# Paged attention with a conditioned residual: scores with the keys on the partitions, sums from a ones column, no maximum, remade tables

## The chip, the cores and the metric

One core of one Trainium2 chip runs the whole program in one launch. The metric is device time in microseconds (us) of one execution; less is better. All tensors are float32.

## The reference, cut to what matters

There are 64 batches of 32 new tokens, width 512. Two residual parts are added to x one after the other: a 32 x 32 mixing of a batch's tokens, chosen by a condition, and grouped-query attention over a paged cache (32 query heads, 8 key/value heads, head width 128, 16 pages of 32 keys for each batch).

```python
x = x + einsum('bct,bcd->bdt', x, L0_weights[condition])
q, k, v = x Wq^T, x Wk^T, x Wv^T            # by heads of 128
q, k = rope(rmsnorm(q) * wq), rope(rmsnorm(k) * wk)   # positions: cached length + 0..31
k_all = concat([k_cache[block_table], k])   # 512 cached keys, 32 new ones
v_all = concat([v_cache[block_table], v])
valid = concat([arange(512) < cached length, ones(32)])
scores = where(valid, q k_all^T / sqrt(128), -1e30)
x = x + (softmax(scores) v_all) Wo^T
```

The conditions, block table and cached lengths (207 to 1644) are inputs; the norm weights lie between 0 and 1; the cached keys and values are normal random numbers.

## The kernel before, in words

The tokens are worked on in 16 tiles of 128 (four batches), and the heads in two halves (four key/value heads, sixteen query heads), so that a half's weights stay on chip: 32 steps, `st.hh` the half and `st.t` the tile. A pair is one batch and one key/value head: 4 query heads x 32 tokens = 128 queries. A step has four batches (`bt`) of four pairs (`g`), 16 slots.

For a pair, `scores` (L407) multiplies the queries (stationary) with 512 cached keys (L414) and 32 new ones (L415) into one PSUM tile, queries on the partitions. One VectorE instruction adds the mask, scales and takes the minimum of the negated scores (L421); ScalarE takes the exponential and the sum (L425); VectorE takes the reciprocal (L427) and multiplies (L428). A slot later `transpose_p` (L431) turns the probabilities over on TensorE, four blocks of 128 keys (L434) and one of 32 (L437), and ScalarE copies them out (L439, L440). Another slot later `values` (L442) multiplies the value tiles (stationary) with them, four times 128 keys (L448) and the 32 new ones (L451), and VectorE copies the output into `ot` (L452).

Beside a step's attention, `pieces` (L469) does the next step's projections, one piece a slot: the mixing (`x1_a`, L251, L271), its transposes (`x1_b`, L274), keys (`k_a`, `k_b`), values (`v_a`) and four groups of queries (`q_a`, `q_b`). Each projection is four matmuls of 512 columns (L303); `norm_rope` (L308) norms and rotates on VectorE with squares on ScalarE (L313) and a power on POOL (L320); `transposed` (L344) turns heads over (L347). `out_proj` (L383, L387) of the step before stands in slot 2.

`load_kv` (L153) fetches a batch's keys by 16 DMAs of one page each on SP's queue (L167; the pages of the input are already stored transposed, 128 x (heads, 32 keys)) and its values by four indirect gathers on POOL's queue (L174). Both tiles have two buffers. Weights come through POOL's queue (L143). The angles' sines and cosines of all tiles are made at the start (L211 to L229). Each engine works in its own order; the order of instructions on it is the framework's, which follows the program with small shifts.

Of the kernel before, what the change touches and what calls it, by code (L numbers as in the profile page):

```python
# [19 lines left out]
P = 128  # L20
B, S, HID = 64, 32, 512  # batches, new tokens of each, width
D, HQ, HK = 128, 32, 8  # head width, query heads, key/value heads
REP = HQ // HK  # query heads to one key/value head
PAGES, PSIZE, NPP = 64, 32, 16
L = NPP * PSIZE  # cached keys that a batch looks at
LK = L + S  # all its keys
NCOND = 16
BT = P // S  # batches in a tile of 128 tokens
NT = B // BT  # tiles of tokens
NHH = 2  # the heads are worked on in two halves, so that a half's weights stay on chip  # L30
GH = HK // NHH  # key/value heads in a half
QH = GH * REP  # query heads in a half
KC = HID // P  # chunks of the width
VC = L // P  # chunks of the cached keys
# [4 lines left out]
PSLOT = P // PSIZE  # pages in a chunk of 128 keys  # L39

TWO_PI = 2.0 * math.pi
C1 = 6.28125  # 2 pi in three parts, the first two short enough for exact products
C2 = float((np.float32(TWO_PI - C1).view(np.uint32) & np.uint32(0xFFFFF000)).view(np.float32))
C3 = TWO_PI - C1 - C2
ROUND = 12582912.0  # 1.5 * 2**23: adding it rounds to an integer
PI_IN = 3.1415925  # the largest float32 below pi
# [3 lines left out]
def cond_resid_paged_attention_kernel(  # L50
    ctx: ExitStack,
    tc: tile.TileContext,
    x: bass.AP,  # [B*S, HID]
    cond: bass.AP,  # [P, NT]: condition of a token's batch
    lens: bass.AP,  # [P, NT]: cached length of a token's batch
    lens_row: bass.AP,  # [1, B]
    pages: bass.AP,  # [B, NPP]: block table
    pages_v: bass.AP,  # [P, B*VC]: page of each cached key, by chunks of 128 keys
    w_cond: bass.AP,  # [NCOND*S, S]
    wq: bass.AP,  # [HID, HQ*D]  # L60
    wk: bass.AP,  # [HID, HK*D]
    wv: bass.AP,  # [HID, HK*D]
    wo: bass.AP,  # [HQ*D, HID]
    qn_w: bass.AP,  # [1, D]
    kn_w: bass.AP,  # [1, D]
    kt: bass.AP,  # [NHH, PAGES, D, GH*PSIZE]: cached keys, transposed page by page
    vc: bass.AP,  # [PAGES*PSIZE*NHH, GH*D]: cached values
    inv_freq: bass.AP,  # [1, D/2]
    out: bass.AP,  # [B*S, HID]
):  # L70
    nc = tc.nc
    HD = D // 2

    def pool(name, bufs, **kw):
        return ctx.enter_context(tc.tile_pool(name=name, bufs=bufs, **kw))

    const = pool("const", 1)
    wpool = pool("weights", 1)
    kv = pool("kv", 2)
    act = pool("act", 2)  # L80
    work = pool("work", 2)
    small = pool("small", 4)
    ps_s = pool("ps_s", 1, space=PSUM)
    ps_t = pool("ps_t", 2, space=PSUM)
    ps_o = pool("ps_o", 2, space=PSUM)
    ps_p = pool("ps_p", 2, space=PSUM)
    dram = pool("dram", 1, space=DRAM)

# [1 line left out]
    cond_sb = const.tile([P, NT], I32, tag="cond", name="cond_sb")  # L90
    nc.sync.dma_start(cond_sb, cond)
    lens_sb = const.tile([P, NT], I32, tag="lens", name="lens_sb")
    nc.sync.dma_start(lens_sb, lens)
# [3 lines left out]
    nc.sync.dma_start(pages_v_sb, pages_v)  # L97
    lens_all_i = const.tile([P, B], I32, tag="lens_all_i", name="lens_all_i")
    nc.sync.dma_start(lens_all_i, lens_row.partition_broadcast(P))

    row_i = const.tile([P, 1], I32, tag="row_i", name="row_i")
    nc.gpsimd.iota(row_i, pattern=[[0, 1]], base=0, channel_multiplier=1)
    nc.vector.tensor_scalar(row_i, row_i, S - 1, None, ALU.bitwise_and)
    row = const.tile([P, 1], F32, tag="row", name="row")  # partition mod 32
    nc.vector.tensor_copy(row, row_i)

    cond_idx = const.tile([P, NT], I32, tag="cond_idx", name="cond_idx")
    nc.vector.tensor_scalar(cond_idx, cond_sb, float(S), row, ALU.mult, ALU.add)
    v_idx = []
    for hh in range(NHH):  # L110
        base = const.tile([P, 1], F32, tag=f"v_base{hh}", name=f"v_base{hh}")
        nc.vector.tensor_scalar(base, row, float(NHH), float(hh), ALU.mult, ALU.add)
        idx = const.tile([P, B * VC], I32, tag=f"v_idx{hh}", name=f"v_idx{hh}")
        nc.vector.tensor_scalar(
            idx, pages_v_sb, float(PSIZE * NHH), base, ALU.mult, ALU.add
        )
        v_idx.append(idx)
# [15 lines left out]
    wt = {}  # L133

    def load_w(kind, hh, g=0):
        if kind == "q":
            src = wq[:, (hh * QH + g * REP) * D : (hh * QH + (g + 1) * REP) * D]
        elif kind == "o":
            src = wo[(hh * QH + g * REP) * D : (hh * QH + (g + 1) * REP) * D, :]
        else:  # L140
            src = (wk if kind == "k" else wv)[:, hh * GH * D : (hh + 1) * GH * D]
        t = wpool.tile([P, 4, 512], F32, tag=f"w{kind}{g}", name=f"w{kind}{g}_{hh}")
        nc.gpsimd.dma_start(t, src.rearrange("(c p) e -> p c e", p=P))  # L143
        wt[kind, g] = t

    def load_x(t):
        xt = work.tile([P, HID], F32, tag="xt", name=f"xt_{t}")
        nc.sync.dma_start(xt, x[t * P : (t + 1) * P, :])
        return xt

    last_k = []

    def load_kv(hh, b):  # L153
        k_t = kv.tile([P, NPP, GH, PSIZE], F32, tag="k_t", name=f"k_t_{hh}_{b}")
        # Behind the last batch's loads: registers hold one batch's page numbers.
        with ExitStack() as order:
            if last_k:
                order.enter_context(tc.issue_after(last_k[0]))
            _, page = nc.values_load_multi_w_load_instructions(
                pages_sb[b : b + 1, :],  # L160
                engines=[mybir.EngineType.SP],
                min_val=0,
                max_val=PAGES - 1,
                skip_runtime_bounds_check_because="a block table names pages of the cache",
            )
        for j in range(NPP):
            ins = nc.sync.dma_start(  # L167
                k_t[:, j, :, :].rearrange("p g r -> p (g r)"),
                kt[hh, bass.ds(page[j], 1)].rearrange("o d e -> (o d) e"),
            )  # L170
        last_k[:] = [ins.ins]
        v_t = kv.tile([P, VC, GH * D], F32, tag="v_t", name=f"v_t_{hh}_{b}")
        for c in range(VC):
            nc.gpsimd.indirect_dma_start(  # L174
                out=v_t[:, c, :],
                out_offset=None,
                in_=vc,
                in_offset=bass.IndirectOffsetOnAxis(
                    ap=v_idx[hh][:, b * VC + c : b * VC + c + 1], axis=0
                ),  # L180
            )
        return k_t, v_t

    load_cond_weights(0)
    x_next = load_x(0)
    load_w("k", 0)
    load_w("v", 0)
    for g in range(GH):
        load_w("q", 0, g)

# [1 line left out]
    norm_w = {}  # L192
    for name, src in (("q", qn_w), ("k", kn_w)):
        w = const.tile([P, D], F32, tag=f"norm_{name}", name=f"norm_{name}")
        nc.sync.dma_start(w, src.partition_broadcast(P))
        norm_w[name] = w
    freq = const.tile([P, HD], F32, tag="freq", name="freq")
    nc.sync.dma_start(freq, inv_freq.partition_broadcast(P))

    pos = const.tile([P, NT], F32, tag="pos", name="pos")  # L200
    nc.vector.tensor_copy(pos, lens_sb)
    nc.vector.tensor_scalar(pos, pos, row, None, ALU.add)
    lens_all = const.tile([P, B], F32, tag="lens_all", name="lens_all")
    nc.vector.tensor_copy(lens_all, lens_all_i)

# [3 lines left out]
    nc.vector.memset(half_pi, math.pi / 2)  # L209

    tmp0 = kv.tile([P, 2, NT * HD], F32, tag="k_t", name="trig_tmp0")  # L211
    tmp1 = kv.tile([P, 2, NT * HD], F32, tag="v_t", name="trig_tmp1")
    ang, turns, red = tmp0[:, 0, :], tmp0[:, 1, :], tmp1[:, 0, :]
    for t in range(NT):
        nc.vector.tensor_scalar(
            ang[:, t * HD : (t + 1) * HD], freq, pos[:, t : t + 1], None, ALU.mult
        )
    nc.vector.tensor_scalar(turns, ang, 1.0 / TWO_PI, ROUND, ALU.mult, ALU.add)
    nc.vector.tensor_scalar(turns, turns, ROUND, None, ALU.subtract)
    nc.vector.scalar_tensor_tensor(red, turns, -C1, ang, ALU.mult, ALU.add)  # L220
    nc.vector.scalar_tensor_tensor(red, turns, -C2, red, ALU.mult, ALU.add)
    nc.vector.scalar_tensor_tensor(red, turns, -C3, red, ALU.mult, ALU.add)
    nc.vector.tensor_scalar(red, red, PI_IN, -PI_IN, ALU.min, ALU.max)
    nc.scalar.activation(sin.rearrange("p t f -> p (t f)"), red, AF.Sin)
    mag = tmp1[:, 1, :]
    nc.scalar.activation(mag, red, AF.Abs)
    nc.scalar.activation(
        cos.rearrange("p t f -> p (t f)"), mag, AF.Sin, bias=half_pi, scale=-1.0
    )  # L229

# [333 lines left out]
```

## Time and profile before

| | |
|---|---|
| median of 3 runs | 2848.94 us (2848.51 to 2850.21) |
| profiled execution, span from first to last instruction | 2849.0 us |
| granted TensorE clock, mean | 0.995 |
| from L387 of one step to L387 of the next, first half / second half | 87.54 / 86.29 us |
| busy of L448 / L414 / L434 / L451 (TensorE) | 594.0 / 560.1 / 314.6 / 247.4 us |
| mean of L425 (ScalarE), L421, L428 (VectorE) | 748, 722, 518 ns |
| first matmul | 22.17 us |
| DMA moved | 326.46 MB, mean 115 GB/s |

The profile is one execution. Engines are PE (TensorE matmul), PEld (TensorE weight load), DVE (VectorE), ACT (ScalarE), POOL (GpSimd) and SP (the queue that issues most DMAs). Part 2 of the page cuts the span into 40 slices, a digit being the busy share in tenths. The chain that ended last goes back from the last instruction, at each step to what released it, and gives shares of the span by engine and by line. The timeline lists instructions with their start, duration and count; matmuls are pipelined, so their durations overlap, and the distance between starts is the pace. The view of waits says who waited for whom: total us, times, longest.

### The profile page before, as it was taken

To read this page: it belongs to the slowest core of one execution; us is meant where nothing else is said; L and a number is where in the kernel's file an instruction comes from. 1 tells how busy PE (TensorE), PEld (TensorE's weight loads), DVE (VectorE), ACT (ScalarE), POOL (GpSimd) and SP (SyncE) were. 2 spreads that over 40 slices of the span, in tenths; PEclk is the share of its full clock that TensorE was granted. 3 is DMA by queue.
4 is the path that set the end of the run, shared out by engine and by line. 5 is a ranking of instruction groups with operands and counts; after the bars stand their busy time and mean duration, and the time that the engine had idled before them with its cause. 6 is when DMAs were issued, how large, how long until landed. Compare 5 with 4: busy or idle time off the path is not lost.

```text
span 2849.0 us, 42362 instructions
## 1 busy us (share of the span) xinstructions
PE 2793.8 (98%) x13024; PEld 1769.4 (62%) x13024; DVE 1445.3 (51%) x4020; ACT 992.9 (35%) x2421; POOL 849.5 (30%) x1052
## 2 busy tenths in 40 slices
PE   3999999999999999999999999999999999999999
PEld 1566666666666666666666666666666666666666
DVE  3545554545554555544555544455544555444553
ACT  1333343333433333333334333334333333333332
POOL 6222322332322223223333222232232232222231
PEclk8999999999999999999999999999999999999999
DMA  6233433334433334335554333334333343333342
GB/s 232 74 110 106 115 110 103 103 111 116 120 90 114 107 114 115 102 101 156 149 165 131 99 111 111 111 111 118 103 106 113 111 118 110 101 109 111 111 115 69
DMA packets 361058, 326.46 MB, mean 115 GB/s; under 512 B 45824, under 2 KB 308608, under 8 KB 360832
## 3 DMA queue, kind: packets, MB, share of 16 engines
q1 hardware_dynamic: 309824, 159.87, 19.6%
q0 software_dynamic: 51008, 163.88, 19.3%
q8 instruction: 104, 1.70, 0.3%
q14 instruction: 122, 1.00, 0.1%
HBM read 302.60 MB, written 12.58 MB: 111 GB/s over the span
## 4 chain that ended last, share of the span: by engine, by line
PE 97%; POOL 1%; DVE 1%; issue 1%; DMA 0%; ACT 0%; SPq 0%; ACTq 0%; DVEq 0%; POOLq 0%
PE ps L414 18%; PE po L448 17%; PE pp_q L303 16%; PE pout L387 16%; PE ppt L434 8%; PE po L451 7%; PE pp_k L303 4%; PE pp_v L303 4%; PE ps L415 3%; PE pt_q L347 2%; PE po L437 2%; PE pmix L271 1%; PE pt_k L347 1%; POOL w_sel L126 0%; POOL v_t L174 0%
## 5 line engine op out<-in xcount | busy, mean ns | idle before, releaser
L174 POOL DMA_INDIRECT v_t<-in_vc_dram,v_idx x512 | 519.3, 1014 | 684.2 <-PE po L448 542.1
L448 PE MATMUL po<-pts,v_t 128*128 128x128 f32 x4096 | 594.0, 279 | 1.4 <-ACT pts L440 1.4
L439 ACT COPY pts<-ppt 128x512 f32<-128x512 f32 x512 | 298.5, 583 | 760.0 <-PE ppt L434 743.6
L414 PE MATMUL ps<-k_t,qt 128*128 128x512 f32 x1024 | 560.1, 629 | 0.0
L448 PEld LDWEIGHTS po<-pts,v_t 128*128 128x128 f32 x4096 | 519.2, 191 | 37.6 <-issue 15.1
L425 ACT ACTIVATE sm<-sm,nm 128x544 f32<-128x544 f32 x512 | 383.1, 748 | 350.4 <-DVE nm L421 343.1
L421 DVE CUSTOM_DVE_ANT_0 sm<-ps,mask 128x544 f32<-128x544 f32 x512 | 369.9, 722 | 253.4 <-PE ps L415 250.5
L303 PE MATMUL pp_q<-wq,x1t 128*128 128x512 f32 x1024 | 474.7, 607 | 0.0
L387 PE MATMUL pout<-wo,ot 128*128 128x512 f32 x1024 | 451.8, 596 | 0.0
L387 PEld LDWEIGHTS pout<-wo,ot 128*128 128x128 f32 x1024 | 190.7, 190 | 221.2 <-issue 221.0
L434 PEld LDWEIGHTS ppt<-ident,sm 128*128 128x128 f32 x2048 | 250.7, 147 | 118.0 <-issue 106.7
L434 PE MATMUL ppt<-ident,sm 128*128 128x128 f32 x2048 | 314.6, 276 | 0.0
L303 PEld LDWEIGHTS pp_q<-wq,x1t 128*128 128x128 f32 x1024 | 186.6, 192 | 186.1 <-issue 186.1
L415 PEld LDWEIGHTS ps<-kn,qt 128*128 128x128 f32 x1024 | 184.8, 190 | 185.1 <-issue 185.1
L428 DVE TENSOR_SCALAR sm<-sm,rden 128x544 f32<-128x544 f32 x512 | 265.2, 518 | 16.4
L452 DVE COPY ot<-po 128x128 f32<-128x128 f32 x512 | 146.2, 285 | 224.4 <-PE po L451 218.4
L320 POOL TENSOR_TENSOR rs_q<-ms_q,minus_half 128x4 f32<-128x4 f32 x128 | 130.7, 1021 | 425.9 <-DVE ms_q L318 425.7
L451 PE MATMUL po<-pts,vn_b 32*128 32x128 f32 x1024 | 247.4, 321 | 0.0
L317 DVE TENSOR_REDUCE ms_q<-sq_q 128x4 f32<-128x512 f32 x128 | 87.8, 686 | 242.1 <-ACT sq_q L313 204.1
L394 DVE TENSOR_TENSOR acc<-pout,acc 128x512 f32<-128x512 f32 x32 | 22.1, 692 | 353.2 <-PE pout L387 353.2
L451 PEld LDWEIGHTS po<-pts,vn_b 32*128 32x128 f32 x1024 | 149.7, 182 | 67.3 <-issue 13.1
L427 DVE RECIPROCAL rden<-den 128x1 f32<-128x1 f32 x512 | 82.4, 161 | 207.8 <-ACT sm L425 207.3
(87 smaller groups left out, 2357.3 us busy)
## 6 DMA issues: line engine op xcount, KB each, us to landing
k_t<-in_kt_dram SPq DMA_DIRECT2D x2048, 64.0 KB
wq<-in_wq_dram POOLq DMA_DIRECT2D x8, 1024.0 KB
wo<-in_wo_dram POOLq DMA_DIRECT2D x8, 1024.0 KB
v_t<-in_vc_dram,v_idx POOLq DMA_INDIRECT x512
vn_b<-vn POOLq DMA_DIRECT2D x128, 64.0 KB
xt<-in_x_dram SPq DMA_DIRECT2D x16, 256.0 KB
x1t_d<-x1t SPq DMA_DIRECT2D x16, 256.0 KB
acc_d<-acc SPq DMA_DIRECT2D x16, 256.0 KB
```

What stands on the lines that cost most here:

```text
L174: nc.gpsimd.indirect_dma_start(out=v_t[:, c, :], out_offset=None, in_=vc, in_offset=bass.IndirectOffsetOnAxis(ap=v_idx[hh][:, b * VC + c : ...
L303: nc.tensor.matmul(pp, st.x1t[:, c, :], w[:, c, :], start=(c == 0), stop=(c == KC - 1))
L387: nc.tensor.matmul(po, st.ot[:, h, :], wt["o", h // REP][:, h % REP, :], start=(h == 0), stop=(h == QH - 1),)
L414: nc.tensor.matmul(ps[:, 0:L], q, k_t[:, :, g, :], start=True, stop=True)
L415: nc.tensor.matmul(ps[:, L:LK], q, st.kn[:, g, bt * S : (bt + 1) * S], start=True, stop=True)
L421: nc.vector.tensor_tensor_reduce(pr.p, ps, mask, -SCALE, 3.0e38, ALU.add, ALU.min, nm)
L425: nc.scalar.activation(pr.p, pr.p, AF.Exp, bias=nm, scale=-1.0, accum_out=den)
L428: nc.vector.tensor_scalar(pr.p, pr.p, rden, None, ALU.mult)
L434: nc.tensor.transpose(pt[:, c, :], pr.p[:, c * P : (c + 1) * P], ident)
L439: nc.scalar.copy(pr.pt[:, 0:VC, :], pt)
L448: nc.tensor.matmul(o, pr.v_t[:, c, d], pr.pt[:, c, :], start=(c == 0), stop=False)
L451: nc.tensor.matmul(o, pr.vn_b[:, d], pr.pt[0:S, VC, :], start=False, stop=True)
```

## The change

The whole kernel is written anew around other layouts; projections, norms, rotation and output projection are the same instructions.

- **Scores transposed.** `scores` takes 128 cached keys at a time as the stationary operand and the pair's 128 queries as the moving one, four times, so the keys lie on the partitions. ScalarE takes the exponential straight from PSUM, without maximum and without mask. `new_scores`, once a batch, multiplies all 128 new keys of the tile with the queries of the four heads; a bias of -1e30 takes out the other batches' keys.
- **Ones column.** The value rows have a 129th column of ones for each head, so that `values` (probabilities stationary, values moving, 129 columns) gives output and denominator. Cached keys past the length are gathered from a row of zeros (`ZROW`). VectorE divides two heads at once, `turn` turns a batch's four outputs over on TensorE and copies them into `ot`.
- **Tables.** `table_piece` reads the cache of a half in 16 pieces, puts a page's keys in the order (key, head), adds the ones column to the values, and writes both to DRAM (`k_tab`, `v_tab`). The first half's pieces stand before step 0, the second half's in steps 4 to 11, two each. The first four batches are read from the inputs and permuted on chip (`direct`).
- **Checked fallback.** At the end all reciprocals of denominators are held against 1e-15 and 1e15; if one is outside, `run(True)` does the work again, in the manner of the kernel before.
- **Queues and order.** The first half's weights come through ScalarE's queue instead of POOL's, the next half's through POOL's in the last step of the first (`next_half`). Angles are made for tile 0 first. `out_proj` stands in slot 3, and `q_b` of a group three slots behind its `q_a`. The scores' PSUM has two buffers, the projections' three.

```diff
+            k_t = kv.tile([P, L, GH], F32, tag="k_t", name=f"k_t_{hh}_{b}_{uid}")
+            if direct:
+                k_raw = wpool.tile([P, NPP, GH, PSIZE], F32, tag="wo2", name=f"k_raw_{b}")
+                k_to, k_from = k_raw.rearrange("p j g r -> p j (g r)"), kt[hh]
+            else:
+                k_to, k_from = k_t.rearrange("p (j r) g -> p j (r g)", j=NPP), k_tab[hh]
...
+            if direct:
+                permuted(k_t.rearrange("p (j r) g -> p j r g", j=NPP), k_raw)
+            else:
+                for c in range(VC):
+                    nc.gpsimd.indirect_dma_start(
+                        out=v_t[:, c, :, :].rearrange("p g d -> p (g d)"),
...
+        def permuted(to, by_head):
+            nc.vector.tensor_copy(to, by_head.rearrange("p j g r -> p j r g"))
+
+        def table_piece(hh, i):
+            n = PAGES // PIECES
+            raw = work.tile([P, n, GH, PSIZE], F32, tag="stage", name=f"traw{hh}_{i}")
+            nc.sync.dma_start(
+                raw.rearrange("p j g r -> p j (g r)"),
+                kt[hh, i * n : (i + 1) * n].rearrange("j d e -> d j e"),
+            )
+            per = work.tile([P, n, PSIZE, GH], F32, tag="stage", name=f"tper{hh}_{i}")
+            permuted(per, raw)
+            nc.sync.dma_start(
+                k_tab[hh][i * n : (i + 1) * n].rearrange("j d e -> d j e"),
+                per.rearrange("p j r g -> p j (r g)"),
+            )
+            st = work.tile([P, GH, D + 1], F32, tag="stage", name=f"tab{hh}_{i}")
+            nc.gpsimd.memset(st[:, :, D : D + 1], 1.0)
+            nc.sync.dma_start(
+                st[:, :, 0:D],
+                vc.rearrange("(p k h) (g d) -> h k p g d", p=P, h=NHH, g=GH)[hh, i],
+            )
+            nc.sync.dma_start(
+                v_tab[hh][0:ZROW, :].rearrange("(p k) e -> k p e", p=P)[i],
+                st.rearrange("p g d -> p (g d)"),
+            )
...
-        nc.tensor.matmul(ps[:, 0:L], q, k_t[:, :, g, :], start=True, stop=True)
-        nc.tensor.matmul(
-            ps[:, L:LK], q, st.kn[:, g, bt * S : (bt + 1) * S], start=True, stop=True
-        )
...
-        nc.vector.tensor_tensor_reduce(
-            pr.p, ps, mask, -SCALE, 3.0e38, ALU.add, ALU.min, nm
-        )
...
-        nc.scalar.activation(pr.p, pr.p, AF.Exp, bias=nm, scale=-1.0, accum_out=den)
...
-        nc.vector.tensor_scalar(pr.p, pr.p, rden, None, ALU.mult)
...
+        def scores(ba, g):
+            ps = ps_s.tile([P, VC, P], F32, tag="ps", name=f"ps_{ba.name}_{g}")
+            for c in range(VC):
+                nc.tensor.matmul(
+                    ps[:, c, :],
+                    ba.k_t[:, c * P : (c + 1) * P, g],
+                    queries(ba, g),
+                    start=True,
+                    stop=True,
+                )
+            pr = work.tile([P, VC, P], F32, tag="pr", name=f"pr_{ba.name}_{g}", bufs=3)
+            nc.scalar.activation(pr, ps, AF.Exp, scale=SCALE)
+            ba.pr[g] = pr
+
+        def new_scores(ba):
+            ps = ps_n.tile([P, GH, P], F32, tag="psn", name=f"psn_{ba.name}")
+            for g in range(GH):
+                nc.tensor.matmul(
+                    ps[:, g, :], ba.st.kn[:, g, :], queries(ba, g), start=True, stop=True
+                )
+            ba.pn = work.tile([P, GH, P], F32, tag="pn", name=f"pn_{ba.name}")
+            nc.scalar.activation(
+                ba.pn, ps, AF.Exp, bias=new_bias[:, ba.bt : ba.bt + 1], scale=SCALE
+            )
...
-            nc.tensor.transpose(pt[:, c, :], pr.p[:, c * P : (c + 1) * P], ident)
...
-        nc.scalar.copy(pr.pt[:, 0:VC, :], pt)
...
-                o, pr.v_t[:, c, d], pr.pt[:, c, :], start=(c == 0), stop=False
...
-        nc.tensor.matmul(o, pr.vn_b[:, d], pr.pt[0:S, VC, :], start=False, stop=True)
...
+            for c in range(VC):
+                nc.tensor.matmul(
+                    o, ba.pr[g][:, c, :], ba.v_t[:, c, g, :], start=(c == 0), stop=False
+                )
+            nc.tensor.matmul(
+                o, ba.pn[:, g, :], ba.st.vn[:, g, :], start=False, stop=True
+            )
...
+            if g % 2:
+                rd = rden[:, ba.n, g - 1 : g + 1]
+                nc.vector.reciprocal(rd, ba.po[:, :, D])
+                nc.vector.tensor_tensor(
+                    ba.o[:, g - 1 : g + 1, :],
...
+        def turn(ba):
+            pt = ps_p.tile([P, GH, P], F32, tag="pp", name=f"pot_{ba.name}")
+            for g in range(GH):
+                nc.tensor.transpose(pt[:, g, :], ba.o[:, g, :], ident)
+            nc.vector.tensor_copy(
+                ba.st.ot[:, :, ba.bt * S : (ba.bt + 1) * S],
+                pt.rearrange("p g (h s) -> p (g h) s", h=REP),
+            )
...
+        load_w("k", 0, eng=nc.scalar)
+        load_w("v", 0, eng=nc.scalar)
...
+        for i in range(PIECES):
+            table_piece(0, i)
...
+            if st.n in range(4, 12):
+                table_piece(1, 2 * (st.n - 4))
+                table_piece(1, 2 * (st.n - 4) + 1)
...
+    redo = const.tile([1, 1], I32, tag="redo", name="redo")
+    run(False)
+    again = nc.values_load(redo[0:1, 0:1])
+    with tc.If(again > 0):
+        run(True)
```

## The prediction

> **What bounds the kernel now.** I read the page from the top: busy shares, the 40 slices, then the chain of work that ended last.
>
> ```profile
> PE 2793.8 (98%) x13024; PEld 1769.4 (62%) x13024; DVE 1445.3 (51%) x4020; ACT 992.9 (35%) x2421; POOL 849.5 (30%) x1052
> ...
> PE   3999999999999999999999999999999999999999
> ...
> DMA  6233433334433334335554333334333343333342
> ...
> PE 97%; POOL 1%; DVE 1%; issue 1%; DMA 0%; ACT 0%; SPq 0%; ACTq 0%; DVEq 0%; POOLq 0%
> PE ps L414 18%; PE po L448 17%; PE pp_q L303 16%; PE pout L387 16%; PE ppt L434 8%; PE po L451 7%; PE pp_k L303 4%; PE pp_v L303 4%; PE ps L415 3%; PE pt_q L347 2%; PE po L437 2%; PE pmix L271 1%; PE pt_k L347 1%; POOL w_sel L126 0%; POOL v_t L174 0%
> ```
>
> The reader is to see that TensorE is never idle after the first slice, and that the chain is TensorE alone. Only 55 us (2849.0 - 2793.8) have no matmul. So a VectorE or ScalarE instruction that goes is worth nothing by itself, and the change is to be priced in TensorE instructions. The timeline of TensorE in mid-run (start, duration; durations overlap, so I take the distance from one start to the next) gives the price of each:
>
> ```profile
> 1505.46 1.13 PE L414 MATMUL ps<-k_t,qt 128*128 128x512 f32 x2
> 1506.42 0.30 PE L415 MATMUL ps<-kn,qt 128*128 128x32 f32 x2
> 1506.56 0.63 PE L347 MATMUL pt_k<-ident,rope_k 128*128 128x128 f32 x4
> 1507.03 0.60 PE L434 MATMUL ppt<-ident,sm 128*128 128x128 f32 x4
> 1507.47 0.27 PE L437 MATMUL po<-ident,sm 128*32 128x128 f32 x1
> 1507.58 1.06 PE L448 MATMUL po<-pts,v_t 128*128 128x128 f32 x8
> 1508.57 0.48 PE L451 MATMUL po<-pts,vn_b 32*128 32x128 f32 x2
> 1508.98 1.12 PE L414 MATMUL ps<-k_t,qt 128*128 128x512 f32 x2
> ...
> 1524.45 0.83 PE L448 MATMUL po<-pts,v_t 128*128 128x128 f32 x6
> 1525.22 0.48 PE L451 MATMUL po<-pts,vn_b 32*128 32x128 f32 x2
> ```
>
> Every float32 matmul is two instructions, a transpose is one. One pair (four query heads of one batch against one key/value head) costs 0.96 (L414) + 0.14 (L415) + 0.44 (L434) + 0.11 (L437) + 0.99 (L448) + 0.41 (L451) = **3.05 us**. Eight L448 take 0.99, six take 0.77: 0.110 us for each, and 0.11 that goes with the change to the 32-row matmul of L451, whose two take 0.205 each. Sixteen pairs are 48.8 us of a step; the step is 87.54 us in the first half of the heads (distance of two runs of L387 in the chain by time, 341.25 to 428.79), so projections, output and their transposes take the other 38.7, and the change leaves these as they are.
>
> **The change on TensorE, for each pair.** Scores: four matmuls of 128 moving columns in place of one of 512, eight instructions. I take 0.110 each, L448 being the row with the same shape and a new stationary tile each time: 0.88. New keys: one matmul against all 128 tokens of the tile, two instructions: 0.22. Values: five matmuls of 129 columns, all 128 rows deep, ten instructions at 0.110 x 129/128: 1.11; the 32-row matmul and its change-over go. The five transposes of the probabilities go; one transpose of the output comes: 0.11. Sum **2.32 us**, 0.73 less, times 512 pairs = **374 us off**. By the quickest row (transposes, 0.44/4 = 0.1075, for all 21) it would be 2.26, 31 us better; by L448's mean in the chain (17.0% of 2849.0 over 4096 = 0.118) 2.47, 77 us worse.
>
> One operand has no row in this trace: the stationary keys of the scores are now read with a step of four floats (16 bytes), since the table holds the four heads side by side. All stationary tiles of before lie densely (qt, v_t, sm, x1t, ot). Bounds: nothing (a spread-out read has no reason to be quicker than a dense one), or the pace of L451, the nearest row at which a matmul of 128 columns does not get its weights in time: 0.205, so 0.095 x 4096 = 389 us more. I take nothing: L434's stationary tile is fetched in 147 ns (mean) and L448's in 191 ns, both at a pace of 0.11, so a load may last longer than the pace and still be covered by earlier ones. [...]
>
> **Beside TensorE.** VectorE loses L421, L427, L428, L452 and the masks (722 + 161 + 518 + 285 ns a pair, 500 a batch), and gains per two pairs a reciprocal and a 256-element product, per batch one 512-element copy; ScalarE loses L439 and L440 and gains one more exponential a batch. Both were under 52% busy; worth nothing. The exponential (748 ns for 544 elements) of a pair has the values of the last pair and the scores of the next before it is wanted, 1.11 + 0.88 = 1.99 us. The pieces of the next step move to other slots, a head's norm and its transposes three slots apart instead of one; the idle time they could save is the 25 us before L347, most of it in the start. The key loads wait, in SP's view, for buffers rather than the other way round:
>
> ```profile
> SPq L167 <- PE ps L415: 945.9, 123, 14.0
> ```
>
> That is 946 us in which SP stood waiting for TensorE to free a key tile, so a step shorter by 12 us (0.73 x 16) is still fed; DMA goes from 38% to some 45% of its engines.
>
> **The tables.** 32 pieces: load 256 KB, permute on VectorE (0.68, as L337's 512 elements), write, and the same for values without the permute. With two stage buffers the next load waits for the last write. The final output DMA takes about 2.6 us (issued 2846.04, span ends 2849.0), the first DMA in the chain 4.9 (lens_all_i): a piece lasts 2.6 + 0.7 + 2.6 = 6 to 4.9 + 0.7 + 4.9 = 10.5 us. The first four batches do without tables, at the price of VectorE's permute of 2048 elements (some 2.7 us) and four multiplies (0.5 each) a batch. The first half's 16 pieces take 95 to 170 us from about 30 us on, and the fifth batch reads them. Before then TensorE has 16 pairs (37), the next step's projections (some 24) and what the built order puts ahead of the fifth batch's scores: an output projection (13.8), two projections (7), new-key scores; the first scores come at 53 us today, so it arrives at about 145 us. Queued behind these waits: on SP the keys of batches 2 to 4, interleaved with pieces; on VectorE the norms and output copies of steps 0 and 1, which TensorE wants. I take **15 us** of stall, bounds 0 and 70. The second half's pieces, two a step in steps 4 to 11, stand in SP's slack (946 us): 0, if that cover fails up to 10 a step (one piece's duration), 80 in all.
>
> **Start.** The weights move from POOL's queue to ScalarE's, and ScalarE's copy of x1t stands behind the issue of the last query weight, its first square behind that of wo; each waits for a lane that an earlier weight holds. The trace moved 284 GB/s in its first 22 us, so 6 to 8 MB land at 21 to 28 us; the copy ended at 26.8 before. Against that only one tile's sine table is made first, not sixteen (12 us of VectorE ahead of the first projection), and 55 us are idle in the start to be had. I take 0, bounds -30 and +20.
>
> **End.** Two comparisons and a sum over 512 counters (0.5 to 0.7 each), a matmul, a flag read by every engine and a branch: **5 us**, bounds 3 and 10. All engines wait for it, nothing is queued behind it, and the last output DMA runs beside it.
>
> **Sum.** 2849.0 - 374 + 15 + 0 + 5 = **2495 us**; the span stands 0.06 us from the median of the runs, 2848.94, so no correction.
>
> **The forecast and its rivals.**
> (A) The forecast, with the bounds of pace, stall and start: 2440 to 2560. For it: same shapes at a known pace, on the engine that is the chain. 62%.
> (B) The strided keys cost in part, half of the upper bound: 2495 + 195 = 2690. 13%.
> (C) The strided keys cost all of it: 2495 + 389 = 2884, **slower** by 1.2%. It decides from a pace of the score instructions of 0.110 + (2849 - 2495)/4096 = 0.196 us. For it: a load of 191 ns that could no longer overlap; against it: nothing in the trace is strided so, either way. 12%.
> (D) The tables are the bound of the first steps and disturb SP in steps 4 to 11: 70 - 15 + 80 more, about 2630. For it: SP and VectorE take their work in order; against it: the 946 us. 8%.
> (E) The change does not do what it says: a denominator leaves 1e-15 to 1e15 and the exact path runs too: some 2495 + 2900 or more, about 5400. Against it: queries are normalised, with weights between 0 and 1, so a score of 128 products over the root of 128 is of the order of one, and 500 such exponentials sum to hundreds. 3%.
> The rest, 2%, is no change.
>
> About 0.2% is what a measurement of this kernel can tell from no change. Faster by more: A, B and D, 0.83; within: 0.02; slower: C and E, 0.15. The range takes A and D and, with B, must hold 8 in 10: 2440 to 2700.
>
> **What would show it.** Right: the new score line at 0.110 from start to start with PE still over 95%, a step of about 75.8 us (87.54 - 11.7), 128x128 transposes of probabilities gone, idle TensorE only before the fifth batch, a few us of branch at the end. Wrong: a weight load of the scores well above 191 ns with a pace near 0.2 (B, C); gaps of TensorE put down to the table's DMAs or to VectorE's permute (D); lines of the exact path in the trace (E). A step of 75.8 with a longer whole would put the miss in start and tables alone.

## The result and the profile after

The change makes the kernel slower. Median of four runs 2968.96 us (2967.63 to 2969.91) against 2849.57 us (2848.51 to 2850.43) for before on the same chip: ratio **1.0416**, interval 1.0401 to 1.0431. The forecast was 2495. The profiled execution of after took 2968.81 us, its span 2967.0, against 2849.0 before: 118.0 us more.

The page of after, in the parts that answer to those shown of before (busy shares, TensorE's and DMA's slices, the chain by engine and by line):

```profile
PE 2897.4 (98%) x14050; PEld 2269.6 (76%) x14050; DVE 846.9 (29%) x2073; ACT 599.8 (20%) x1020; POOL 814.6 (27%) x949
...
PE   4989999999999999999999999999999999999998
...
DMA  8654555543333334335454333333333333333331
...
PE 95%; DMA 2%; POOL 1%; issue 1%; DVE 1%; SPq 0%; ACT 0%; DVEq 0%; ACTq 0%; POOLq 0%
PE ps_x L573 32%; PE po_x L602 15%; PE pout_x L527 14%; PE pp_q_x L446 14%; PE po_x L605 4%; PE psn_x L588 4%; PE pp_k_x L446 3%; PE pp_v_x L446 3%; PE pt_q_x L490 2%; PE pot_x L624 2%; DMA tab<-in_vc_dram 1%; DMA v_tab<-tab 1%; POOL w_sel L116 1%; PE pt_k_x L490 0%; PE pmix_x L410 0%
```

VectorE and ScalarE lost the instructions that the forecast said they would lose (busy 1445 to 847 us, 993 to 600), and it was worth nothing: TensorE is still the chain. The new score line, L573, holds 32% of it, where L414, the scores of before, held 18%. The other number to stop at is PEld, the weight load: 62% before, 76% now. The groups show where it comes from (busy us, mean ns of one; then idle time before, with its releaser):

```profile
L573 PE MATMUL ps_x<-qt_x,k_t_x 128*128 128x128 f32 x4096 | 1049.0, 397 | 12.0 <-DMA k_t_x<-k_tab 10.0
L573 PEld LDWEIGHTS ps_x<-qt_x,k_t_x 128*128 128x128 f32 x4096 | 1000.7, 327 | 15.1 <-issue 13.4
...
L602 PEld LDWEIGHTS po_x<-v_x,pr_x 128*128 128x128 f32 x4096 | 518.1, 192 | 109.2 <-issue 108.6
L602 PE MATMUL po_x<-v_x,pr_x 128*128 128x129 f32 x4096 | 542.2, 275 | 0.3 <-ACT pr_x L581 0.3
```

Both lines are 4096 instructions with a new 128x128 stationary tile each time and 128 or 129 columns moving. The load of the strided keys (L573) lasts 327 ns, that of the dense probabilities (L602) 192. TensorE's timeline in mid-run (start, duration) turns that into a pace; as in the prediction, the distance between starts counts:

```profile
1504.62 0.39 PE L605 MATMUL po_x<-vn_x,pn_x 128*128 128x129 f32 x2
1504.84 2.03 PE L573 MATMUL ps_x<-qt_x,k_t_x 128*128 128x128 f32 x8
1506.70 0.60 PE L490 MATMUL pt_q_x<-ident,rope_q_x 128*128 128x128 f32 x4
1507.14 1.06 PE L602 MATMUL po_x<-v_x,pr_x 128*128 128x129 f32 x8
1508.04 0.39 PE L605 MATMUL po_x<-vn_x,pn_x 128*128 128x129 f32 x2
```

Eight L573 take 1506.70 - 1504.84 = 1.86 us, **0.2325 each**; eight L602 take 0.90, 0.112 each. No stall stands in between: the engine is shown busy all along, and only the distance of the starts shows the slower pace.

By stages, from the chain in order of time: up to the second output projection 269.32 us against 253.72, +15.6; the 29 steps from there to the last output projection but one 2611.6 against 2518.2, +93.4, some +3.2 each; the rest 86.1 against 77.1, +9.0. The sum is 118.0. So 93 of the 118 us are one price paid in every step, and not a stall somewhere; the other 25 lie in the first and the last stretch.

### The profile page after: what moved, and what is told of

Its sections match the earlier page's. It is cut to its first block, busy times and chain, and to the rows that moved or that the text cites. A ratio compares the mean times of both kernels' runs of the same rounds, so it can differ in the third digit from the quotient of the medians.

```text
span 2967.0 us, 41777 instructions
## 1 busy us (share of the span) xinstructions
PE 2897.4 (98%) x14050; PEld 2269.6 (76%) x14050; DVE 846.9 (29%) x2073; ACT 599.8 (20%) x1020; POOL 814.6 (27%) x949
## 4 chain that ended last, share of the span: by engine, by line
PE 95%; DMA 2%; POOL 1%; issue 1%; DVE 1%; SPq 0%; ACT 0%; DVEq 0%; ACTq 0%; POOLq 0%
PE ps_x L573 32%; PE po_x L602 15%; PE pout_x L527 14%; PE pp_q_x L446 14%; PE po_x L605 4%; PE psn_x L588 4%; PE pp_k_x L446 3%; PE pp_v_x L446 3%; PE pt_q_x L490 2%; PE pot_x L624 2%; DMA tab<-in_vc_dram 1%; DMA v_tab<-tab 1%; POOL w_sel L116 1%; PE pt_k_x L490 0%; PE pmix_x L410 0%
## 5 line engine op out<-in xcount | busy, mean ns | idle before, releaser
L573 PE MATMUL ps_x<-qt_x,k_t_x 128*128 128x128 f32 x4096 | 1049.0, 397 | 12.0 <-DMA k_t_x<-k_tab 10.0
L573 PEld LDWEIGHTS ps_x<-qt_x,k_t_x 128*128 128x128 f32 x4096 | 1000.7, 327 | 15.1 <-issue 13.4
L318 POOL DMA_INDIRECT v_x<-v_tab,v_idx x496 | 537.1, 1083 | 1426.5 <-PE po_x L602 1304.7
L581 ACT ACTIVATE pr_x<-ps_x 128x512 f32<-128x512 f32 x512 | 305.3, 597 | 1702.1 <-PE ps_x L573 1702.1
L602 PEld LDWEIGHTS po_x<-v_x,pr_x 128*128 128x128 f32 x4096 | 518.1, 192 | 109.2 <-issue 108.6
L602 PE MATMUL po_x<-v_x,pr_x 128*128 128x129 f32 x4096 | 542.2, 275 | 0.3 <-ACT pr_x L581 0.3
L446 PE MATMUL pp_q_x<-wq_x,x1t_x 128*128 128x512 f32 x1024 | 462.9, 594 | 0.0
L527 PE MATMUL pout_x<-wo_x,ot_x 128*128 128x512 f32 x1024 | 446.7, 594 | 1.7 <-DVE ot_x L625 1.7
L527 PEld LDWEIGHTS pout_x<-wo_x,ot_x 128*128 128x128 f32 x1024 | 193.2, 191 | 232.8 <-issue 230.7
L605 PE MATMUL po_x<-vn_x,pn_x 128*128 128x129 f32 x1024 | 198.2, 275 | 0.0
```

What stands on the lines that cost most here:

```text
L318: nc.gpsimd.indirect_dma_start(out=v_t[:, c, :, :].rearrange("p g d -> p (g d)"), out_offset=None, in_=v_tab[hh], in_offset=bass.IndirectO ...
L446: nc.tensor.matmul(pp, st.x1t[:, c, :], w[:, c, :], start=(c == 0), stop=(c == KC - 1))
L527: nc.tensor.matmul(po, st.ot[:, h, :], wt["o", st.hh, h // REP][:, h % REP, :], start=(h == 0), stop=(h == QH - 1),)
L573: nc.tensor.matmul(ps[:, c, :], ba.k_t[:, c * P : (c + 1) * P, g], queries(ba, g), start=True, stop=True,)
L581: nc.scalar.activation(pr, ps, AF.Exp, scale=SCALE)
L602: nc.tensor.matmul(o, ba.pr[g][:, c, :], ba.v_t[:, c, g, :], start=(c == 0), stop=False)
```

## The experiments

The theory after the result: the stationary read of the keys is what costs, each float of a column lying 16 bytes behind the one before. Rivals: the tables' transfers, the changed order of the work, or any read that is not dense.

**1. The same kernel, keys read densely.** Only the slice of the tile changes, so the instructions, their order and the transfers stay.

```diff
-                    ba.k_t[:, c * P : (c + 1) * P, g],
+                    ba.k_t.rearrange("p l g -> p (l g)")[:, (g * VC + c) * P : (g * VC + c + 1) * P],
```

> The changed kernel with one edit: the stationary tile of the scores is 128 neighbouring floats of the key tile instead of 128 floats with a step of four. It thereby multiplies with keys of mixed heads, so the scores are not the reference's; number, shape and order of all instructions stay. Theory (the step of the stationary read costs): the score line goes from a pace of 0.2325 us to 0.110, its weight load from 327 ns to about 192, 4096 x 0.1225 = 502 us less, but the fifth batch is then reached some 15 us sooner and waits that much longer for the tables: span 2480, faster than before (ratio 0.87). Rival (the pace comes from something else in the new score group: the PSUM tile in four parts, or key tiles that a DMA writes meanwhile): nothing changes, 2967.

Measured: 2503.6 us (2500.79 to 2504.78), ratio to before 0.8772 (0.8757 to 0.8786), span 2503.0. Its score loads among the groups:

```profile
L573 PEld LDWEIGHTS ps_x<-qt_x,k_t_x 128*128 128x128 f32 x4096 | 507.6, 193 | 8.8 <-DMA k_t_x<-k_tab 5.9 <-issue 2.9
```

and its timeline of TensorE:

```profile
1504.88 1.06 PE L573 MATMUL ps_x<-qt_x,k_t_x 128*128 128x128 f32 x8
1505.77 0.60 PE L490 MATMUL pt_q_x<-ident,rope_q_x 128*128 128x128 f32 x4
```

The load falls from 327 to 193 ns, the pace from 0.2325 to 0.111 (0.89/8). 2967.0 - 2503.0 = **464 us** is what the stride costs on balance, and without it the kernel lies 8 us from the forecast's sum. The paces alone would give 0.1215 x 4096 = 498; of the 34 us between, 16 are idle time that the dense kernel has more of on TensorE (85.7 against 69.6 us), and the rest was not traced. A step in the second half is 74.87 us (before 86.29, after 89.52). Tables, order and epilogue cannot be the loss: all of them are still here.

**2 to 4. Other steps of the same read.** Counted in lines of 16 bytes, the unit that the paces below bear out, step two puts two reads on a line (64 lines per tile), step three four reads on three lines (96), steps four and sixteen one read on each (128). A price per line, a price for any step, and a price that grows with the step give different times. (Kernels 2 to 6 were run once each.)

```diff
-                    ba.k_t[:, c * P : (c + 1) * P, g],
+                    ba.k_t.rearrange("p l (a e) -> p (l a) e", e=2)[:, (g * VC + c) // 2 * P : ((g * VC + c) // 2 + 1) * P, c % 2],
```

> As the dense one, but with a step of two floats (8 bytes); scores again of mixed keys. If the load pays for each new line of 16 bytes and two reads of one line hide it: pace 0.110, span 2480. If any step other than one is slow: pace 0.2325, span 2967. If the cost grows evenly with the step: pace about 0.15, span 2640.

```diff
-                    ba.k_t[:, c * P : (c + 1) * P, g],
+                    ba.k_t.rearrange("p l g -> p (l g)")[:, (g * VC + c) % 15 // 3 * 384 : ((g * VC + c) % 15 // 3 + 1) * 384].rearrange("p (l e) -> p l e", e=3)[:, :, c % 3],
```

> As the dense one, with a step of three floats (12 bytes): three lines of 16 bytes for every four reads. Lines: 0.110 if a line each 1.33 reads is hidden in part, up to 0.2 if not, about 0.17 to 0.2 in the middle, span 2720 to 2850. Any step: 0.2325, 2967. Growing evenly with the step: 0.19, 2800.

```diff
-                    ba.k_t[:, c * P : (c + 1) * P, g],
+                    ba.k_t.rearrange("p (l i) g -> p l (i g)", i=4)[:, :, g * VC + c],
```

> As the dense one, with a step of sixteen floats (64 bytes). Lines: a read never shares a line, as with four, so the same 0.2325 and 2967. Growing evenly with the step: far slower, 0.6 or more and a span above 4000. The score group also waits for a batch's whole key tile instead of a quarter, a few us at the first table batch.

The score loads of the three kernels, step two, three and sixteen in turn:

```profile
L573 PEld LDWEIGHTS ps_x<-qt_x,k_t_x 128*128 128x128 f32 x4096 | 532.6, 198 | 9.1 <-DMA k_t_x<-k_tab 6.7 <-issue 2.4
```
```profile
L573 PEld LDWEIGHTS ps_x<-qt_x,k_t_x 128*128 128x128 f32 x4096 | 760.6, 261 | 8.4 <-issue 8.4
```
```profile
L573 PEld LDWEIGHTS ps_x<-qt_x,k_t_x 128*128 128x128 f32 x4096 | 938.6, 309 | 15.9 <-issue 15.5
```

With the paces, read from starts in each timeline as above:

| step (floats) | lines | load, ns | pace, us | pace / line, ns | time of the one run, us |
|---|---|---|---|---|---|
| 1 | 32 | 193 | 0.111 | (L602's pace too) | 2503.6 (median) |
| 2 | 64 | 198 | 0.1175 | 1.84 | 2528.23 |
| 3 | 96 | 261 | 0.174 | 1.81 | 2731.02 |
| 4 | 128 | 327 | 0.2325 | 1.82 | 2968.96 (median) |
| 16 | 128 | 309 | 0.219 | 1.71 | 2908.8 |

From step two to four the pace is 1.81 to 1.84 ns for each 16-byte line. With lines of 8 bytes step two would cost as much as four, and it has 0.1175 against 0.2325; with lines of 32 sixteen would cost twice as much as four, and it has 0.219. A price for any step falls with step two (24.6 us for the whole kernel), one that grows with the step falls with sixteen, which is a little quicker than four; why it is, these runs do not show.

**5. The other operand.** In before, the keys are the moving operand of L414; here they are read with the step of four.

```diff
-        nc.tensor.matmul(ps[:, 0:L], q, k_t[:, :, g, :], start=True, stop=True)
+        nc.tensor.matmul(ps[:, 0:L], q, k_t.rearrange("p j g (r e) -> p (j g r) e", e=4)[:, :, g], start=True, stop=True)
```

> The kernel before with one edit: L414's moving operand, 512 keys, is read with a step of four floats (16 bytes) instead of runs of 32; the scores are those of mixed keys, not the reference's. If the 1.82 ns for each new line of 16 bytes, found for the stationary operand, hold for the moving one too, an instruction reads 512 lines in 0.93 us instead of 0.43 to 0.48: 1024 x 0.45 to 0.5 = 460 to 510 us more, span 3310 to 3360. If only the weight load pays for lines: 2849, no change.

Measured: 3322.79 us, span 3321.0. TensorE's timeline of this kernel:

```profile
1501.87 1.96 PE L414 MATMUL ps<-k_t,qt 128*128 128x512 f32 x2
1503.65 0.32 PE L415 MATMUL ps<-kn,qt 128*128 128x32 f32 x2
...
1505.79 2.05 PE L414 MATMUL ps<-k_t,qt 128*128 128x512 f32 x2
1507.65 0.32 PE L415 MATMUL ps<-kn,qt 128*128 128x32 f32 x2
```

Two L414 take 1.78 us here, behind transposes, 0.89 each; behind a 32-row L451, where before has 0.48 (1505.46 to 1506.42), they take 0.93 in this kernel (1505.79 to 1507.65). That is 1.74 to 1.82 ns a line. The moving operand pays about the same price, so in these runs it is not the weight load alone that pays.

**6. The change to 32 rows.** The prediction credited the change with the vanishing 32-row matmul of the new values, at 0.30 us a pair. Here L451 of before gets the 128-row operands of its neighbours, and nothing else changes.

```diff
-        nc.tensor.matmul(o, pr.vn_b[:, d], pr.pt[0:S, VC, :], start=False, stop=True)
+        nc.tensor.matmul(o, pr.v_t[:, 0, d], pr.pt[:, 0, :], start=False, stop=True)
```

> The kernel before with one edit: L451, the new keys' values on 32 rows, is replaced by a matmul on all 128 rows of the first chunk once more; the new keys' part of the output is left out. One part of the change alone: the prediction put the change to 32 rows and back at 0.30 us a pair (0.11 before L451, 0.10 on each of its two instructions). If so: 512 x 0.30 = 154 us less, span 2695. If the extra belongs to the accumulation's end and not to the row count: 2849.

Measured: 2678.83 us, span 2677.1, so 171.9 us less than before, 0.336 a pair. TensorE's timeline of this kernel:

```profile
1501.40 1.06 PE L448 MATMUL po<-pts,v_t 128*128 128x128 f32 x8
1502.29 0.39 PE L451 MATMUL po<-pts,v_t 128*128 128x128 f32 x2
1502.52 1.02 PE L414 MATMUL ps<-k_t,qt 128*128 128x512 f32 x2
1503.38 0.30 PE L415 MATMUL ps<-kn,qt 128*128 128x32 f32 x2
```

L448 0.89 where before had 0.99, L451 0.23 for 0.41, and the next scores 0.86 for 0.96: the 32-row matmul delays what stands ahead of it and behind it by a tenth of a us each. Four times the rows cost less.

**7 and 8. Dense keys with the reference's result.** The dense key tile must come from somewhere. Kernel 7 drops the key tables and lets the key DMAs put each page, as 128-byte runs, in its place in a tile that has the heads apart; kernel 8 fetches pages as they are and has VectorE copy them, head by head, into one such tile. Kernel 7's core (kernel 8 has `nc.vector.tensor_copy(k_t[:, g, :].rearrange("p (j r) -> p j r", j=NPP), k_raw[:, :, g, :])` for each head behind its page DMAs):

```diff
-            k_t = kv.tile([P, L, GH], F32, tag="k_t", name=f"k_t_{hh}_{b}_{uid}")
+            k_t = kv.tile([P, GH, L], F32, tag="k_t", name=f"k_t_{hh}_{b}_{uid}")
...
-                    k_to[:, j, :],
-                    k_from[bass.ds(page[j], 1)].rearrange("o d e -> (o d) e"),
+                    k_t[:, :, j * PSIZE : (j + 1) * PSIZE],
+                    kt[hh, bass.ds(page[j], 1)].rearrange("o d (g r) -> (o d) g r", g=GH),
...
-                    ba.k_t[:, c * P : (c + 1) * P, g],
+                    ba.k_t[:, g, c * P : (c + 1) * P],
```

> The changed kernel without key tables: each page's keys come straight from the input into a key tile by heads (head, key), in runs of 128 bytes, so the scores' stationary tiles are dense. The result is the reference's. If a packet of 128 bytes costs its share of one of 512 bytes (29 ns): the score pace is 0.111, span 2480. If a packet costs the same whatever its size: 1.05 million packets x 29 ns / 16 = 1930 us for the keys, 77% of the span beside 21% for the values, the keys come late, span 2550 to 2700. Either way faster than before.

> The changed kernel without key tables: pages come from the input as they lie (512-byte runs) into one tile, and VectorE permutes them, head by head, into one dense key tile (four copies of 512 elements, 0.55 to 0.65 us each, 2.4 us a batch, 300 us in all on an engine that was busy 841 us). The result is the reference's. Score pace 0.111; span 2470 to 2500 if the single buffers are fed in time (a load has a batch, 18.7 us, for 1 MB), up to 2600 if TensorE waits 1 us a batch for the copies.

Measured: kernel 7 **2510.28 us** (2506.49 to 2514.4), ratio to before 0.8796 (0.8782 to 0.8811); kernel 8 2520.89 (2519.47 to 2531.1), ratio 0.885 (0.8831 to 0.8869). Both beat before and after. The waits before the scores: 26.7 us on key DMAs in kernel 7, 34.9 us on VectorE's copies in kernel 8. The groups of kernel 7:

```profile
L546 PE MATMUL ps_x<-qt_x,k_t_x 128*128 128x128 f32 x4096 | 558.1, 276 | 27.2 <-DMA k_t_x<-in_kt_dram 26.7
```

The short runs are not free elsewhere: one key DMA's issue on SP takes 543 ns (median) against 333 in before, and the next one starts 0.73 us after it (median over the run) against 0.52. Stretches can be slower, as this one of its SP timeline (30 issues in 29.33 us, 0.98 each):

```profile
1499.60 29.33 SPq L298 DMA_DIRECT2D k_t_x<-in_kt_dram  x30
```

Sixteen of them are 11.7 us at the median and 15.6 in such a stretch, and a batch of four pairs lasts 18.7 (74.87/4). It fits, with 3 us or more to spare on the average, though the chain of kernel 7 still follows these issues for 8% of its span.

**9 and 10. Without any tables.** Kernel 9 also drops the value tables: values by sixteen page DMAs a batch on SP beside a standing ones column, the mask as a bias in four exponentials of 128 elements. Kernel 10 keeps kernel 7's keys and gathers the values on POOL straight from the input, without a ones column and a mask, so its result is not the reference's.

```diff
+            for j in range(NPP):
+                nc.sync.dma_start(
+                    k_t[:, :, j * PSIZE : (j + 1) * PSIZE],
+                    kt[hh, bass.ds(page[j], 1)].rearrange("o d (g r) -> (o d) g r", g=GH),
+                )
+                q = j % PSLOT * PSIZE
...
+                    v_t[q : q + PSIZE, j // PSLOT, :, 0:D],
+                    v_in[hh, bass.ds(page[j], 1)].rearrange("o r g d -> (o r) g d"),
```

> The changed kernel without any table and with dense keys: keys as in the run with 128-byte runs; values by 16 DMAs of a page on SP's queue, in runs of 512 bytes, beside a ones column that is set once; the mask of the cached keys is a bias of the exponential, which ScalarE takes in four parts of 128. The result is the reference's. It shows what the tables cost beside the score line. If the wait for the tables and their disturbance of the start are what keeps the dense kernel at 2503: some 15 to 25 us less, 2480 to 2490. If that time belongs to the weights' arrival and the norms of the first step, which stay: 2500. If 32 issues a batch of 0.33 to 0.39 us (12 of the 18.7 us that a batch lasts) make SP the bound, or four exponentials a pair ScalarE: 2550 to 2700.

> The dense kernel with 128-byte key runs, and without tables again, this time with the values gathered on POOL's queue as before the change, 512 floats a row straight from the input; SP issues 16 DMAs a batch, not 32. The value rows have no ones column between the heads, so the denominators are wrong for three heads of four, the cached keys are not masked, and the check's bounds are opened so that it still runs and passes; the number and shape of the matmuls and exponentials stay. It takes away the tables alone, against the run with them (2510). If the tables' reads, writes and waits are what keeps that run above 32 steps of 74.5 us plus start: 2485 to 2500. If the wait is only replaced (by the weights' arrival, the norms of step 0, the keys): 2505 to 2515. If SP is the bound even so (16 issues of 0.98 us are 15.7 of 18.7): 2510 or more, with waits on key DMAs all along the run.

Kernel 9: 2983.39 us (2977.91 to 2989.24), ratio 1.0453 (1.0438 to 1.0467). Its chain by engine, and SP's timeline:

```profile
PE 57%; SPq 27%; issue 7%; DMA 5%; ACT 3%; DVE 1%; ACTq 0%; DVEq 0%
```
```profile
1503.72 9.61 SPq L288 DMA_DIRECT2D v_x<-in_vc_dram  x16
...
1515.74 9.71 SPq L282 DMA_DIRECT2D k_t_x<-in_kt_dram  x10
```

In this stretch 0.60 us for each value issue and 0.97 for each key issue, by the medians of the run 0.51 and 0.73: 16 of each are 20 to 25 us of one queue against 18.7 of TensorE, and a batch took 2987.5/128 = 23.3. So the bound moved to SP. The expectation's case of SP as the bound is what came; the run says nothing of the tables' price.

Kernel 10: 2479.45 us (2478.05 to 2481.29), ratio 0.8688 (0.8673 to 0.8702). Against kernel 7 in the same stretches (length, then busy time and count of PE, PEld, DVE, ACT, POOL, then clock, DMA share, GB/s), first kernel 10, then kernel 7:

```profile
0.00:100.00 100.00, 53.93 (x212) 31.54 (x213) 42.17 (x135) 21.55 (x35) 42.79 (x65) 0.91 0.66 185
100.00:200.00 100.00, 99.55 (x591) 74.04 (x590) 35.49 (x87) 25.15 (x43) 32.57 (x38) 1.00 0.57 119
200.00:300.00 100.00, 100.00 (x637) 77.99 (x636) 36.02 (x92) 27.38 (x47) 36.15 (x42) 1.00 0.62 129
```
```profile
0.00:100.00 100.00, 43.48 (x166) 25.06 (x167) 42.49 (x141) 18.88 (x31) 41.41 (x78) 0.86 0.77 231
100.00:200.00 100.00, 94.16 (x541) 68.36 (x540) 36.48 (x98) 23.73 (x41) 27.69 (x43) 1.00 0.72 168
200.00:300.00 100.00, 90.78 (x516) 66.72 (x515) 30.46 (x75) 22.40 (x38) 31.31 (x43) 0.97 0.70 162
```

TensorE is 10.5, 5.4 and 9.2 us busier in the three stretches: 25 of the **31 us** (2510.28 - 2479.45) that what kernel 10 leaves out (value tables, ones column, mask) costs kernel 7 lie in the first 300 us. A version that keeps the mask and the ones and still needs no table was not tried.

## Why the prediction failed

**The step that failed** is the one operand without a row: "I take nothing: L434's stationary tile is fetched in 147 ns (mean) and L448's in 191 ns, both at a pace of 0.11, so a load may last longer than the pace and still be covered by earlier ones." Two dense loads at one pace show that some 190 ns can be covered; they say nothing of a load that lasts 327. What experiments 1 to 4 put in its place: with 64 to 128 lines of 16 bytes to a read the pace was 1.71 to 1.84 ns a line, and dense, with 32, it was 0.111. With the 128 lines of a step of four it was 0.2325.

**Rival C was right in mechanism and too small in price.** Its upper bound came from L451's pace (0.095 x 4096 = 389); 464 were measured, 0.113 an instruction. L451 was near in shape only: experiment 6 shows that its price is the change to 32 rows and back (0.336 us a pair), another mechanism; that its weights came too late, as the prediction had it, no run shows. The prediction gave the cases with a strided price only 25%, on the strength of two dense rows that did not bear on it.

**The rest of the sum held, in part by luck.** With dense keys it said 2495 and 2503.0 was measured. By term:
- Steps: 374 forecast. The 29 steps between the same output projections take 2180.3 us in experiment 1 against 2518.2, 11.65 each, which over 32 steps is 373. New scores, values, new keys and turn ran at their rows' 0.11; the 32-row change-over, taken as 0.30, was 0.336 a pair.
- Tables: a stall of 15 forecast. TensorE waited in four spells before the first scores of table keys, together the 12.0 us in the group line of L573, 10.0 of them put down to the key DMAs (timeline of after; idle time in brackets). In experiment 1's kernel it was 5.1 us on the keys and 1.8 on the gathered values.

```profile
184.00 1.27 PE L573 MATMUL ps_x<-qt_x,k_t_x 128*128 128x128 f32 x4 [7.21 <-DMA k_t_x<-k_tab]
187.23 1.27 PE L573 MATMUL ps_x<-qt_x,k_t_x 128*128 128x128 f32 x4 [1.96 <-issue]
190.58 1.27 PE L573 MATMUL ps_x<-qt_x,k_t_x 128*128 128x128 f32 x4 [2.08 <-DMA k_t_x<-k_tab]
192.59 1.27 PE L573 MATMUL ps_x<-qt_x,k_t_x 128*128 128x128 f32 x4 [0.73 <-DMA k_t_x<-k_tab]
```

  A piece was forecast at 6 to 10.5 us and, after the first, takes 7 to 11, but in the chain it is the values' path, load then write, that is followed, as in this piece (chain of after, in order of time):

```profile
121.59 0.58 DVE tper L350
122.66 4.02 DMA tab<-in_vc_dram
126.75 5.82 DMA v_tab<-tab
132.69 0.65 DVE tper L350
```

- Start: 0 was taken. The first scores came at 69.16 us, 15.7 later than the 53.5 of before. The wait that the prediction named, ScalarE's copy of x1t behind the weights' issues, is there but made only 2.8 us of it: the first projection began at 29.54 against 26.79. The rest lies before the keys' transposes, for which TensorE waited 14.74 us (1.34 in before). VectorE came to the keys' norm only at 45.73 us, behind the first batches' value products, permutes and more angles, and then waited for a cosine product that POOL made at 49.98 (23.77 in before), behind its gathers of weights and values. The prediction did not count POOL's order; which of the two queues matters more was not tried (timeline of after):

```profile
27.61 1.28 ACT L420 ACT_TABLE_LOAD   x1 [27.61 <-DMA wq_x<-in_wq_dram]
...
49.98 0.31 POOL L436 TENSOR_TENSOR cw_k_x<-norm_k,cos 128x64 f32<-128x64 f32 x1
...
50.33 0.69 DVE L467 TENSOR_TENSOR rope_k_x<-pp_k_x,cw_k_x 128x512 f32<-128x512 f32 x1 [3.92 <-POOL cw_k_x L436]
...
53.79 1.09 PE L490 MATMUL pt_k_x<-ident,rope_k_x 128*128 128x128 f32 x4 [14.74 <-DVE rope_k_x L482]
```

  Steps, start, tables and end together are what was measured: 2849.0 - 373 + 27 = 2503.0, with 20 forecast for the last three. Of the 27, the stretch up to the second output projection (247.05 us in experiment 1) holds 17, with 15 forecast for start and tables. That they agree is in part luck: the first scores came 17.7 us later than in before (71.23), the tables held TensorE up for 7 us and not 15, and 18 us of idle time that before has ahead of later query transposes went away.
- End: 5 forecast. From the last output matmul to the end of the span 12.3 us against 3.7: 8.6, inside 3 to 10.
- The slack of SP held as forecast (its waits in after: us in all, times, longest):

```profile
SPq L308 <- PE ps_x L573: 1083.7, 119, 20.9
```

  1083.7 us of waiting for TensorE to free key tiles, so rival D (the tables as the bound) did not come about. The exact path never ran (rival E).

## What to carry to other kernels

Before an operand of TensorE is laid out anew, count the 16-byte lines that its read touches: for 128 columns of float32 the pace here stayed near the dense 0.111 us at a step of two floats (64 lines, 0.1175), and a step of four doubled it (128 lines, 0.2325, 1.82 ns a line). An operand without a row in the trace deserves its upper bound, and a row that shares the mechanism with it; if none does, the answer needs a run and not a choice. When the layout that suits the DMA is one that TensorE reads slowly, let short DMA runs build the dense tile (kernel 7, runs of 128 bytes: 2510.28 us against 2968.96), and check that the queue which issues them can still follow (kernel 9, 32 issues a batch on SP: 2983.39).

## What was not expected of the hardware

- A busy share does not tell a read that is held up from a matmul: with and without the stride TensorE is shown busy for 98 and 97%; the distance between starts and the mean load (327 against 193 ns) show it.
- A 32-row float32 matmul among 128-row ones costs 0.336 us a pair more than one that is 128 rows deep, in part on its neighbours.
- Page DMAs of 64 KB with runs of 128 bytes keep SP 0.73 us each from issue to issue (median, kernel 7); with 512-byte runs it is 0.52 for the key pages of before and 0.51 for the value pages of kernel 9.
